# Swapping the first two bank products of each pair in a two-layer graph network kernel

## The chip, the cores and the metric

The kernel runs on one core of one Trainium2 chip. The metric is the device time in microseconds (us) from the first to the last instruction of that core, as the median of several runs. The core has five engines that work side by side and wait for one another through semaphores: TensorE (PE in the profile, its weight loads PEld), VectorE (DVE), ScalarE (ACT), GpSimd (POOL) and SyncE (SP), which issues most of the transfers.

## The reference

Input x is 128 graphs of 64 nodes with 768 features each; `adj` is their 0/1 adjacency. Two layers follow one another, each added to its input. Cut to what matters:

```python
# layer 0: relational graph layer
h = jnp.maximum(_layernorm(x), 0.0)
ctx = jnp.matmul(adj, h @ Wadj.T + badj) / deg            # neighbours
ctx = ctx + jnp.matmul(radj, h @ Wrev.T + brev) / rdeg    # neighbours the other way
ctx = ctx + h @ Wself.T + bself                           # the node itself
rel = agg @ Wr.T + br * deg + ragg @ Wrr.T + brr * rdeg   # sums of relation embeddings
x = x + ctx + rel
# layer 1: graph attention with 6 heads of 128, tanh scores, softmax over neighbours, gate
h = jnp.maximum(_layernorm(x), 0.0)
x = x + gate * elu(attention(h)) + (1 - gate) * h
```

The change touches layer 0 alone, and in it the three products with `Wadj`, `Wrev` and `Wself`.

## The kernel before

The 8192 rows are cut into 64 tiles of 128 rows, and the tiles into 32 pairs. Pass 1 does layer 0 pair by pair, pass 2 does layer 1. In pass 1 the product of a pair (2 tiles by 768 features) with the weights (768 by 768) is split into blocks: 2 tiles by 3 parts of the inner dimension (operands a00 to a12), and 3 by 3 blocks of weights (b00 to b22). Eighteen block products would be needed. The kernel needs fifteen: it forms sums of operands (f1 to f11) and sums of weights (g1 to g14), and adds or subtracts the running content of a PSUM bank to or from the output blocks after each product.

Each line of the table is one product: operand, weights, bank, whether it begins the bank anew, output block, sign, and whether the table products of the relation part are added too. Bank a holds a chain of seven products that is never cleared within a pair; after every product the bank's running sum is read.

```python
PRODUCTS = (
    ("f1", "g6", "a", True, "11", "+", False),
    ("f7", "g10", "b", True, "00", "-", False),
    ("a01", "b11", "d", True, "01", "+", True),
    ("f4", "b21", "a", False, "01", "-", False),
    ("a00", "g12", "b", False, "01", "-", False),
    ("f3", "g8", "c", True, "12", "-", False),
    ("a02", "g14", "a", False, "00", "-", False),
    ("f9", "g9", "b", False, "02", "+", False),
    ("f11", "b10", "d", True, "00", "+", True),
    ("f6", "g5", "a", False, "02", "+", False),
    ("f8", "g3", "b", False, "12", "-", False),
    ("f10", "b12", "c", False, "02", "+", True),
    ("f5", "b22", "a", False, "12", "-", False),
    ("a11", "g1", "b", False, "11", "+", True),
    ("f2", "g11", "a", False, "10", "+", True),
)
# pair 0 uses plain block products instead, in the banks "abcdab", and so ends in bank b
PLAIN = tuple((f"a{k}{j}", f"b{j}{q}", "abcdab"[2 * i + k], j == 0, f"{k}{q}" if j == 2 else None,
               "+", i > 0) for i, q in enumerate((0, 2, 1)) for k in range(2) for j in range(3))
```

How the steps of one pair come about. `psw` is a pool of PSUM tiles with one buffer for each bank's name, so a bank that begins anew must first have been read to the end.

```python
def main(p):
    ...
    def new(b):
        bank[b] = psw.tile([P, 512], F32, name=f"pw{b}")

    def counts(b, c, first=False):          # the table products: two matmuls (L617)
        ...
    def add(b, c, sign="+"):
        ...
        if sign == "+":
            nc.vector.tensor_add(v, bank[b][:, :CQ], v)        # L625
        else:
            nc.vector.tensor_sub(v, v, bank[b][:, :CQ])        # L627

    def product(an, bn, b, first, c, sign, cnt):
        def step(q, s):
            if first and q == s == 0:
                new(b)
            nc.tensor.matmul(bank[b][:, :CQ], OPS[p, an][:, q, s, :], bw[bn][...], ...)   # L633
            if q == KQ - 1 and s == 2 and c:
                if cnt:
                    counts(b, c)
                add(b, c, sign)
        for q in range(KQ):         # 2
            for s in range(3):      # Wadj, Wrev, Wself
                steps.append(lambda q=q, s=s: step(q, s))

    for x in PRODUCTS if p else PLAIN:
        product(*x)

    rest_of = ["12"] if p else ["00", "10"]
    for i, c in enumerate(rest_of):
        b = "dc"[i % 2]
        steps.append(lambda b=b, c=c: (counts(b, c, True), add(b, c)))
    return steps
```

A product is six steps. Other work is put in between by the number of the step, always in the same place in the order of instructions, whichever products stand there:

```python
def beside(p):
    ends = [f for k in range(2) for f in finish(p - 1, k)]
    steps = [(0, lambda: form(p, "f5", "f6", "f3")), (10, lambda: form(p, "f10")),
             (18, lambda: form(p, "f11"))]
    steps += list(zip((32, 40, 49, 55), ends))
    if p == 1:
        steps += [(8, lambda: weights_sums("g9")), (25, lambda: weights_sums("g1")), ...]
    if p + 1 == NP:
        return steps + fetch()      # the last pair: weights of pass 2 are loaded over those of pass 1
    n = p + 1
    return steps + [
        (7, lambda: prep(n)),       # the two casts of the next pair's adjacency
        (13, lambda: devs(n)),
        ...
        (53, lambda: form(n, "f1")),
        ...
        (66, lambda: form(n, "f7", "f4")),
        ...
        (77, lambda: form(n, "f8", "f9", "f2")),
        ...]
```

Each engine runs its instructions in the order in which the program issues them.

Of the kernel before, what the change touches and what calls it, by code (L numbers as in the profile page):

```python
# [53 lines left out]
# [9 lines that stand above are left out]
# [10 lines left out]
PLAIN = tuple((f"a{k}{j}", f"b{j}{q}", "abcdab"[2 * i + k], j == 0, f"{k}{q}" if j == 2 else None,  # L73
               "+", i > 0) for i, q in enumerate((0, 2, 1)) for k in range(2) for j in range(3))
# [58 lines left out]
def kernel(  # L133
# [56 lines left out]
    NP = NT // 2  # L190
# [35 lines left out]
    def merged(main, side):  # L226

        side = sorted(side, key=lambda e: e[0])
        i = 0
        for n, step in enumerate(main):  # L230
            while i < len(side) and side[i][0] <= n:
                side[i][1]()
                i += 1
            step()
        for _, step in side[i:]:
            step()
# [117 lines left out]
    with ExitStack() as px:  # L354
# [249 lines left out]
        def main(p):  # L604

            bank = {}
            steps = []

            def new(b):
                bank[b] = psw.tile([P, 512], F32, name=f"pw{b}")  # L610

            def counts(b, c, first=False):
                k, q = int(c[0]), int(c[1])
                if first:
                    new(b)
                for i, (a, e) in enumerate(PARTS):
                    nc.tensor.matmul(bank[b][:, :CQ], CT_T[p, k][: 3 * (e - a), i, :],  # L617
                                     tabs[i][:, q * CQ : (q + 1) * CQ],
                                     start=(first and i == 0), stop=True, skip_group_check=True)

            def add(b, c, sign="+"):
                k, q = int(c[0]), int(c[1])
                v = X[2 * p + k][:, q * CQ : (q + 1) * CQ]
# [9 lines that stand above are left out]
                    nc.tensor.matmul(  # L633
                        bank[b][:, :CQ], OPS[p, an][:, q, s, :],
                        bw[bn][:, (s * KQ + q) * CQ : (s * KQ + q + 1) * CQ],
                        start=(first and q == s == 0), stop=(q == KQ - 1 and s == 2),
                        skip_group_check=True)
# [4 lines that stand above are left out]
                for q in range(KQ):  # L642
                    for s in range(3):
                        steps.append(lambda q=q, s=s: step(q, s))

            for x in PRODUCTS if p else PLAIN:
                product(*x)

            rest_of = ["12"] if p else ["00", "10"]
# [4 lines that stand above are left out]
# [144 lines left out]
        for p in range(NP):  # L798
            merged(main(p), beside(p) if p else first)
# [436 lines left out]
```

## Time and profile before

| what | value |
|---|---|
| time, median of 3 runs | 2499.7 us (2497.94 to 2507.48) |
| span of the profiled run | 2494.1 us |
| TensorE busy | 2458.7 us, 99% |
| VectorE busy | 1998.9 us, 80% |
| ScalarE busy | 1074.4 us, 43% |
| GpSimd busy | 449.2 us, 18% |
| mean granted TensorE clock | 0.998 |
| busy between 60 and 1500 us, of 1440 | TensorE 1431.2 us, VectorE 1095.0 us |

The profile is one execution, seen by the hardware profiler. Pass 1 takes the first 1500 us or so, pass 2 the rest. In each line of a timeline stand the start, the duration, the engine, the line of the kernel, the operation, and the tiles written and read; several equal instructions in a row are merged into one line with their number. `pwa` to `pwd` are the PSUM banks a to d of pass 1, `op` and `oq` its operands, `x` the rows to which results are added. A matmul of 32-bit data shows as two records. The end of a matmul is modelled, its start is recorded.

### The profile page before, as it was taken

How to read it: one execution, taken by the hardware profiler on the slowest of the kernel's cores; microseconds unless marked ns; L12 is line 12 of the kernel's file. 1: busy time of each engine (PE TensorE's matmuls, PEld its weight loads, DVE VectorE, ACT ScalarE, POOL GpSimd, SP SyncE). 2: the span in 40 equal slices, each digit the busy share in tenths (PEclk: the TensorE clock that was granted, in tenths of full speed). 3: DMA queues.
4: the chain of work that ended last, by engine and by line, in shares of the span. 5: the costliest groups of instructions: out<-in, count | busy, mean ns of one | idle time of the engine just before them, and what ended most of it. 6: DMA issues, size and time to landing. Idle time of an engine off the chain costs nothing. (4 is left out here: it accounts for less than half of the span.)

```text
span 2494.1 us, 35435 instructions
## 1 busy us (share of the span) xinstructions
PE 2458.7 (99%) x12108; PEld 1724.9 (69%) x12108; DVE 1998.9 (80%) x4105; ACT 1074.4 (43%) x3591; POOL 449.2 (18%) x799
## 2 busy tenths in 40 slices
PE   8999999999999999999999999999999999999997
PEld 6888888888888888888888884444444444444445
DVE  8877777777777777777777766888888888888889
ACT  2122122122122222222222224777777777777777
POOL 1112112112111121121121121111111111111122
PEclk9999999999999999999999999999999999999999
DMA  5112112112122122122122154344444444444434
GB/s 178 55 53 106 53 60 100 53 66 93 54 72 87 53 74 85 53 79 81 54 88 72 53 174 140 94 110 111 109 104 110 104 104 104 107 113 105 104 85 100
DMA packets 116215, 224.58 MB, mean 90 GB/s; under 512 B 36554, under 2 KB 49981, under 8 KB 116034
## 3 DMA queue, kind: packets, MB, share of 16 engines
q1 hardware_dynamic: 106162, 197.50, 24.4%
q0 software_dynamic: 9728, 24.78, 6.2%
q8 instruction: 95, 1.56, 0.3%
q14 instruction: 86, 0.70, 0.1%
q10 hardware_dynamic: 144, 0.04, 0.0%
HBM read 96.07 MB, written 100.66 MB: 79 GB/s over the span
## 5 line engine op out<-in xcount | busy, mean ns | idle before, releaser
L633 PE MATMUL pwa<-weights,op 128*128 128x256 f32 x2304 | 548.9, 383 | 10.6 <-DVE x L625 8.8
L633 PEld LDWEIGHTS pwa<-weights,op 128*128 128x128 f32 x2304 | 417.4, 190 | 79.3 <-DVE x L625 17.3
L633 PE MATMUL pwb<-weights,op 128*128 128x256 f32 x1536 | 360.7, 381 | 0.0
L633 PEld LDWEIGHTS pwb<-weights,op 128*128 128x128 f32 x1536 | 289.1, 190 | 44.9 <-issue 6.7
L889 PE MATMUL pma<-weights,op_f 128*128 128x512 f32 x620 | 307.7, 593 | 0.6 <-DVE weights L916 0.6
L286 POOL TENSOR_TENSOR rn<-ve,mhalf 128x1 f32<-128x1 f32 x128 | 93.7, 732 | 948.6 <-DVE ve L285 948.5
L307 DVE TENSOR_TENSOR op<-op 128x768 f32<-128x768 f32 x248 | 241.3, 993 | 1.2
L941 ACT ACTIVATE pr<-pr 128x128 f32<-128x128 f32 x768 | 225.4, 296 | 25.3 <-DVE pr L931 25.2
L483 ACT ACTIVATE h<-x,rn 128x768 f32<-128x768 f32 x64 | 62.4, 1022 | 399.8 <-DVE rn L290 380.9
L663 ACT ACTIVATE hf<-x,rn 128x768 f32<-128x768 f32 x64 | 65.7, 1027 | 353.7 <-issue 250.1
L594 ACT COPY op<-pb 128x768 f32<-128x768 f32 x160 | 121.1, 797 | 180.9 <-PE pb L586 180.3
L889 PE MATMUL pmb<-weights,op_f 128*128 128x512 f32 x372 | 191.2, 595 | 0.0
L889 PEld LDWEIGHTS pma<-weights,op_f 128*128 128x128 f32 x620 | 111.8, 190 | 113.2 <-issue 104.3
L633 PE MATMUL pwc<-weights,op 128*128 128x256 f32 x780 | 187.0, 383 | 0.0
L633 PE MATMUL pwd<-weights,op 128*128 128x256 f32 x768 | 176.3, 379 | 0.0
L633 PEld LDWEIGHTS pwc<-weights,op 128*128 128x128 f32 x780 | 145.6, 190 | 25.2 <-issue 6.7
L665 POOL TENSOR_TENSOR x<-x,hf 128x768 f32<-128x768 f32 x64 | 136.1, 2127 | 134.9 <-ACT hf L663 134.9
L633 PEld LDWEIGHTS pwd<-weights,op 128*128 128x128 f32 x768 | 145.8, 190 | 20.0 <-issue 0.2
L586 PE MATMUL pb<-r,h 64*128 64x192 f32 x1536 | 151.8, 337 | 0.4 <-ACT h L483 0.4
L625 DVE TENSOR_TENSOR x<-pwa,x 128x256 f32<-128x256 f32 x95 | 40.0, 422 | 134.2 <-PE pwa L617 78.4
L586 PEld LDWEIGHTS pb<-r,h 64*128 64x128 f32 x1536 | 122.9, 187 | 33.9 <-issue 22.7
L941 ACT ACTIVATION_READ_ACCUMULATOR pr<-pr 128x1 f32 x768 | 144.4, 188 | 0.0
(207 smaller groups left out, 4337.6 us busy)
## 6 DMA issues: line engine op xcount, KB each, us to landing
x<-in_x_dram SPq DMA_DIRECT2D x64, 384.0 KB
h<-hf SPq DMA_DIRECT2D x64, 384.0 KB
out_dram<-x SPq DMA_DIRECT2D x64, 384.0 KB
hh<-hh SPq DMA_DIRECT2D x64, 384.0 KB
h<-h SPq DMA_DIRECT2D x64, 384.0 KB
x<-hh SPq DMA_DIRECT2D x64, 384.0 KB
out_dram<-f POOLq DMA_DIRECT2D x62, 384.0 KB, 5.0
hx<-weights SPq DMA_DIRECT2D x88, 192.0 KB
```

The source lines that it names most:

```text
L286: nc.gpsimd.tensor_tensor(to[:, 0:1], ve, mhalf, op=OP.pow)
L307: return (nc.vector.tensor_add if s1 == "+" else nc.vector.tensor_sub)(to, x, y)
L483: nc.scalar.activation(h, X[t], AF.Relu, scale=to[:, 0:1], bias=to[:, 1:2])
L586: nc.tensor.matmul(ps[:, g, i * 3 * N : (i + 1) * 3 * N], H0[t][s, kb * P : (kb + 1) * P], rts[p % 2][s, k].rearrange("p s n -> p (s n)"), ...
L594: nc.scalar.copy(a.rearrange("p h s (g n) -> p g (h s) n", g=GT), ps[:, :, : 6 * N].rearrange("p g (x n) -> p g x n", n=N))
L625: nc.vector.tensor_add(v, bank[b][:, :CQ], v)
L633: nc.tensor.matmul(bank[b][:, :CQ], OPS[p, an][:, q, s, :], bw[bn][:, (s * KQ + q) * CQ : (s * KQ + q + 1) * CQ], start=(first and q == s ...
L663: nc.scalar.activation(h, X[t], AF.Relu, scale=to[:, 0:1], bias=to[:, 1:2])
L665: nc.gpsimd.tensor_add(X[t], X[t], h)
L889: nc.tensor.matmul(bank[p, b], OPS[p, an][:, q, :], bw2[bn][:, 2 * q * CQ : 2 * (q + 1) * CQ], start=(first and q == 0), stop=(q == KQ - 1 ...
L941: nc.scalar.activation(PR[t][:, j, h, :], PR[t][:, j, h, :], AF.Copy, accum_out=to)
```

## The change

The first product of a pair goes into bank a and the second into bank b. The pair before has just ended in bank a. The change lets those two products change places, so that bank b comes first, and does so in pairs 1 to 30. Pair 0 has its own table, and the last pair keeps its order, since the loads for pass 2 overwrite the weights g6 as soon as its first product is through. It is meant to give VectorE the length of a product to read bank a before TensorE writes to it again.

```diff
-            for x in PRODUCTS if p else PLAIN:
+
+
+            later = (PRODUCTS[1], PRODUCTS[0], *PRODUCTS[2:]) if p + 1 < NP else PRODUCTS
+            for x in later if p else PLAIN:
                 product(*x)
```

## The prediction

> **What bounds the kernel now.** I began with the page's first part and its slices. TensorE is busy for 2458.7 of 2494.1 us, so the end of the kernel is set by how closely TensorE's work is packed, and only two things can move it: less work for TensorE, or fewer holes between its matmuls. The change keeps every matmul, so I looked for holes. The page's list of costly groups names one that repeats. In each line the last two fields are the group's busy time with the mean of one, then the idle time just before the group and what ended it.
>
> ```profile
> PE 2458.7 (99%) x12108; PEld 1724.9 (69%) x12108; DVE 1998.9 (80%) x4105; ACT 1074.4 (43%) x3591; POOL 449.2 (18%) x799
> ...
> L633 PE MATMUL pwa<-weights,op 128*128 128x256 f32 x2304 | 548.9, 383 | 10.6 <-DVE x L625 8.8
> L633 PEld LDWEIGHTS pwa<-weights,op 128*128 128x128 f32 x2304 | 417.4, 190 | 79.3 <-DVE x L625 17.3
> ```
>
> L633 is the matmul of pass 1's products, L625 is the addition by which VectorE reads a finished bank. Of all of pass 1's matmuls, those into bank a wait, and mostly for one kind of VectorE instruction. The view of waits, asked for TensorE between 60 and 1480 us (pairs 1 to 30 and the ends of their neighbours), has a single line:
>
> ```profile
> PE pwa L633 <- DVE x L625: 8.8, 30, 0.3
> ```
>
> That is the total, the number of waits and the longest: 30 waits of 0.3 us. To see where they fall I read the timeline of TensorE around one boundary between two pairs. The columns are start, duration, line and operation, output and inputs, and in brackets the idle time before.
>
> ```profile
> 720.59 0.39 PE L617 MATMUL pwa<-tab,cntT 126*128 126x256 bf16 x2
> 720.81 0.38 PE L617 MATMUL pwd<-tab,cntT 126*128 126x256 bf16 x2
> 721.49 2.86 PE L633 MATMUL pwa<-weights,op 128*128 128x256 f32 x12 [0.29 <-DVE x L625]
> 724.18 2.75 PE L633 MATMUL pwb<-weights,op 128*128 128x256 f32 x12
> 726.77 2.75 PE L633 MATMUL pwd<-weights,op 128*128 128x256 f32 x12
> 729.36 0.39 PE L617 MATMUL pwd<-tab,cntT 126*128 126x256 bf16 x2
> 729.59 1.03 PE L633 MATMUL pwa<-weights,op 128*128 128x256 f32 x4
> ```
>
> A product is six matmuls, which the trace shows as 12 records. The old pair ends with its product f2 x g11 and two table matmuls into bank a, then two table matmuls into bank d. The new pair's first product, f1 x g6, goes into bank a again, and must wait until VectorE has read that bank. The next product, f7 x g10 into b, waits for nothing. VectorE over the same time:
>
> ```profile
> 721.01 0.42 DVE L625 TENSOR_TENSOR x<-pwa,x 128x256 f32<-128x256 f32 x1 [2.56 <-PE pwa L617]
> 721.35 0.41 DVE L625 TENSOR_TENSOR x<-pwd,x 128x256 f32<-128x256 f32 x1
> 721.68 0.95 DVE L305 SCALAR_TENSOR_TENSOR op<-op 128x768 f32<-128x768 f32 x1
> 722.66 1.83 DVE L307 TENSOR_TENSOR op<-op 128x768 f32<-128x768 f32 x2
> 724.41 0.42 DVE L625 TENSOR_TENSOR x<-pwa,x 128x256 f32<-128x256 f32 x1
> 724.81 0.29 DVE L488 CAST af<-ai 128x256 f32<-128x256 int32 x1
> 725.14 0.29 DVE L490 CAST ab<-af 128x256 bf16<-128x256 f32 x1
> 725.35 0.95 DVE L307 TENSOR_TENSOR op<-op 128x768 f32<-128x768 f32 x1
> 726.97 0.42 DVE L627 TENSOR_TENSOR x<-x,pwb 128x256 f32<-128x256 f32 x1 [0.67 <-PE pwb L633]
> ```
>
> VectorE was idle for 2.56 us before it read bank a at 721.01, so it is not late: the wait is the length of its own read (0.42 us) and the signals on both sides, of which the two table matmuls into d cover only 0.22 us.
>
> **What the Trainium skill says.** "PSUM — Partial Sum Buffer", section "PSUM bank collisions raise a hardware error", says that two engines must not use one bank and quadrant of partitions at once, at whichever addresses, and that the program must guard it with semaphores by bank. So the wait cannot just be dropped; another bank must be worked on meanwhile, which is the change. The trace agrees in so far as TensorE resumes at 721.49, after the read's 721.43. "TensorE: Matmul & The Clock Gate", section "Step-by-step: what each phase is for", says that weight loads are pulled ahead of running matmuls and that the drain of one matmul overlaps the fill of the next, so a wait costs more than the hole one sees. The trace agrees: the hole is 0.29 us, but the weight loads waited 17.3 us over 30 times, 0.58 us each. Section "HAM oscillation — how this bites in real kernels" of the same page puts the idle gap that slows the clock at about 3.4 us. Here gaps are 0.3 us and the granted clock is 0.998, so I count no gain from the clock.
>
> **The change part by part.** No instruction is added or removed. For pairs 1 to 30 the first product goes into b and the second into a.
>
> What one wait costs, from starts. With no wait, the two table matmuls and the next product's start are 729.59 - 729.36 = 0.23 us apart, and a product takes 726.77 - 724.18 = 2.59 us to the start of the next. At the boundary the two distances are 721.49 - 720.81 = 0.68 and 724.18 - 721.49 = 2.69 us. So 0.45 us are lost ahead of the product and 0.10 us inside it, because its first weight load could not run beside earlier work: 0.55 us in all. The boundary to the last pair shows the same: 1464.98 - 1461.61 = 3.37 us from the table matmuls into d to the second product, as 724.18 - 720.81 = 3.37 here, against 0.23 + 2.59 = 2.82.
>
> Where it goes away. The 30 waits are at the starts of pairs 2 to 31. The last pair, 31, keeps its order, so 29 waits go: 29 x 0.55 = 16.0 us.
>
> What is there in its place for bank b. It was last read at 718.03 (0.42 us), well before 721.03, when f7 x g10 can now start. Its operand f7 was formed at about 755 to 757 us in the cycle before the boundary at 767.79, some 11 us ahead, so no operand is missing.
>
> Where it costs. Pair 0 has another order of banks: it ends in bank b, with four table matmuls into d and c behind it. There the present order is the free one and the new one waits:
>
> ```profile
> 72.95 0.38 PE L617 MATMUL pwd<-tab,cntT 126*128 126x256 bf16 x2
> 73.17 0.39 PE L617 MATMUL pwc<-tab,cntT 126*128 126x256 bf16 x2
> 73.39 2.75 PE L633 MATMUL pwa<-weights,op 128*128 128x256 f32 x12
> ```
>
> VectorE reads b at 73.34. At the other boundary TensorE resumed 721.49 - 721.01 = 0.48 us after such a read began, which here gives 73.82, 0.43 us later than 73.39; with the 0.10 us inside the product the cost is 0.53 us, once.
>
> What moves later. Bank a's second product of the pair, f4 x b21 (729.59 here), must wait for the read of f1 x g6, and that read moves from first to second place on VectorE. With the swap, f7 x g10 ends at about 723.6 and is read at about 724.4, when VectorE is through with its three formed operands (the read of bank a stood there before). f1 x g6 runs from 723.6 to about 726.2. VectorE comes from its casts and one more formed operand at about 726.3, reads a, and is done by 726.9. The product f4 x b21 is due at 729.0. Two microseconds are left. In pair 1 an extra sum of weights (1.75 us) stands between the two reads: bank b was read there at 80.45 to 80.86, and bank a will be instead, against a start of f4 x b21 near 81.9. About one microsecond is left.
>
> Sum: 16.0 - 0.5 = 15.5 us of TensorE's path. VectorE has 23% to 25% idle in this pass (1095.0 of 1440.0 us busy between 60 and 1500) and sits waiting for TensorE before most of its reads, so it follows a TensorE that is 0.55 us a pair earlier. Pass 2 is the same program and only starts sooner. 2499.7 - 15.5 = 2484.2 us.
>
> **The rivals.**
> The first: only the visible holes go, 29 x 0.29 = 8.5 us, and 2491 us remain. For it speaks that busy time on TensorE is modelled; against it that starts are recorded and give 0.55 us twice over.
> The second: the wait moves to f4 x b21, since bank a now has one product less between its two uses. For it speaks that VectorE reads it in order behind operands and casts. Against it stand the 2 us of slack above; it would need VectorE to be 2 us later than now. If it came true in all pairs, the gain would shrink towards nothing and the time would stay at 2500.
> The third: TensorE comes so early that an operand or a buffer from ScalarE or VectorE becomes its bound, say the three formed operands at the pair's start. Against it: TensorE now waits for nothing else in these pairs, and the first of the three is used in the sixth product, more than 10 us after the boundary. It would cost a few tenths a pair, ending near 2490.
>
> **Range and chances.** The sum of 15.5 us has an error of perhaps 1 us from reading starts to 0.01 us at a few boundaries. Most of the range is the spread of runs: 2497.94, 2499.7 and 2507.48 before. A median of the changed kernel may sit 3 us either side, and I leave more room above for a part of the rivals: 2479.5 to 2490.5. A change of 2% is 50 us, more than three times all that the removed waits hold, so within 2% is nearly certain.
>
> **What would show it right or wrong.** Right: TensorE's wait for L625 falls from 30 times to about two (start of pair 1 on bank b, start of pair 31 on bank a), some 0.6 us in all, and the weight loads' wait falls from 17.3 us to about 1.2. A pair takes 45.75 us instead of 46.30 ((1462.29 - 721.49) / 16). The starts at a boundary stand 0.23 us and 2.59 us apart. Wrong: a new wait for L625 before the fourth product, a wait of the same size on bank b at each boundary, or a pair that keeps 46.3 us without a hole that one can see. A drop of the granted clock below 0.998 would also spoil it.

## The result and the profile after

The changed kernel takes 2484.24 us (median of 4 runs, 2481.44 to 2486.32) against 2501.7 us for the kernel before in the same series (the three runs given above and a fourth at 2503.71). The ratio is 0.9927 with a 95% interval of 0.9904 to 0.9951, which is 12 to 24 us less. 2484.2 us was predicted. Three later series of the kernel before, of 28, 20 and 9 runs, have medians of 2498.96, 2499.61 and 2499.79 us. Two of the four runs before lie above 2503 us, but only 11 of these 57, so the gain is more likely 15 than 17 us. (The description of the kernel above speaks of seven products in bank a; its table has six.)

From the page of the changed kernel: TensorE's share, and the groups of matmuls and weight loads of bank a, now with bank b's beside them.

```profile
PE 2455.3 (99%) x12108; PEld 1727.7 (70%) x12108; DVE 1998.9 (80%) x4105; ACT 1074.4 (43%) x3591; POOL 449.9 (18%) x799
...
L633 PE MATMUL pwa<-weights,op 128*128 128x256 f32 x2304 | 547.7, 382 | 3.7 <-DVE x L627 3.4
L633 PEld LDWEIGHTS pwa<-weights,op 128*128 128x128 f32 x2304 | 420.9, 190 | 66.7 <-issue 7.6
...
L633 PE MATMUL pwb<-weights,op 128*128 128x256 f32 x1536 | 360.8, 381 | 0.3 <-DVE x L625 0.3
```

Bank a's 8.8 us behind L625 are gone from its group. What is left there is a single wait of 3.4 us behind another line, L627, and L625 no longer ends most of the idle time of bank a's weight loads. The view of waits for TensorE between 60 and 1480 us has two lines now:

```profile
PE pwa L633 <- DVE x L625: 0.3, 1, 0.3
PE pwb L633 <- DVE x L625: 0.3, 1, 0.3
```

They are the start of the last pair, which keeps its order, and the start of pair 1, where the new order waits. TensorE's timeline at a boundary between two pairs:

```profile
714.07 0.39 PE L617 MATMUL pwd<-tab,cntT 126*128 126x256 bf16 x2
714.29 2.75 PE L633 MATMUL pwb<-weights,op 128*128 128x256 f32 x12
716.88 2.75 PE L633 MATMUL pwa<-weights,op 128*128 128x256 f32 x12
...
722.06 0.39 PE L617 MATMUL pwd<-tab,cntT 126*128 126x256 bf16 x2
722.28 1.03 PE L633 MATMUL pwa<-weights,op 128*128 128x256 f32 x4
```

The first product starts 0.22 us after the table matmuls and gives way to the next after 2.59 us: 2.81 us where it was 3.37 us. VectorE beside it:

```profile
714.26 0.42 DVE L625 TENSOR_TENSOR x<-pwa,x 128x256 f32<-128x256 f32 x1 [2.56 <-PE pwa L617]
...
717.66 0.41 DVE L627 TENSOR_TENSOR x<-x,pwb 128x256 f32<-128x256 f32 x1
...
719.67 0.42 DVE L625 TENSOR_TENSOR x<-pwa,x 128x256 f32<-128x256 f32 x1 [0.19 <-PE pwa L633]
720.01 1.01 DVE L282 BATCH_NORM_STATS2 st<-x 128x6 f32<-128x384 f32 x2
```

The read of the old pair's bank a still starts as soon as its table matmuls are through, but TensorE works in bank b meanwhile. The read of the new a is over at 720.09; f4 x b21 needs bank a at 722.28. The start of pair 1 shows the price:

```profile
73.17 0.38 PE L617 MATMUL pwc<-tab,cntT 126*128 126x256 bf16 x2
73.83 2.86 PE L633 MATMUL pwb<-weights,op 128*128 128x256 f32 x12 [0.27 <-DVE x L625]
```

The product starts at 73.83 instead of 73.39 us, and takes 2.69 us to the next one's start (76.52).

Where the time went, by landmarks. The first stretch runs from the last two table matmuls of pair 0 to the first product of pair 31, the second from there to the first product of pass 2 into its bank d (`pmd`), both from starts in the timelines of one profile. The medians come from four series of runs (the changed kernel; the next three; the four with sums or tail up to tail_sums; tail_sums_w), and each ratio is against the kernel before in the same series, so kernels of different series are compared by their ratios. The names of the rows are those of the experiments below.

| kernel | median us | ratio, 95% interval | pairs 1 to 30, us | last pair, us |
|---|---|---|---|---|
| before | 2501.7 | 1 | 1462.29 - 73.17 = 1389.12 | 1506.37 - 1462.29 = 44.08 |
| changed | 2484.24 | 0.9927 (0.9904 to 0.9951) | 1446.58 - 73.17 = 1373.41 | 1494.30 - 1446.58 = 47.72 |
| d_first | 2511.52 | 1.005 (1.0034 to 1.0067) | 1399.51 | 48.60 |
| devs_early | 2499.35 | 1.0005 (0.9996 to 1.0014) | 1387.37 | 49.79 |
| half | 2491.46 | 0.997 (0.9962 to 0.9978) | 1380.70 | 46.25 |
| before_sums | 2495.42 | 0.9986 (0.9978 to 0.9993) | 1389.11 | 42.01 |
| after_sums | 2479.5 | 0.9924 (0.9912 to 0.9937) | 1373.39 | 41.85 |
| tail | 2484.11 | 0.9938 (0.9925 to 0.9951) | 1372.43 | 45.32 |
| tail_sums | 2478.51 | 0.9913 (0.99 to 0.9927) | 1372.42 | 43.09 |
| tail_sums_w | 2478.27 | 0.992 (0.9906 to 0.9933) | 1372.42 | 41.91 |
| before, second and third profile | | | 1389.11, 1389.11 | 45.03, 44.54 |
| changed, second and third profile | | | 1373.41, 1373.42 | 45.86, 46.44 |

The first stretch repeats to 0.02 us from profile to profile, the second does not. The change took 15.71 us from the first stretch. In these two profiles the last pair gave 3.64 us back, so pass 2 began 12.07 us earlier. Pass 2 keeps this lead until some 22 us before its end (a matmul at 2472.05 us before is at 2459.98 us after), and 1.7 us go in those last 22 us, where the granted clock was 0.50 for longer (from 2461.20 us, for 10.24 us, in place of 3.41 us, and in both kernels again in the last 7.47 us). That leaves the 10.4 us between the two spans (2494.1 and 2483.7).

### The profile page after: what moved, and what is told of

Read it like the earlier page. It is cut to its first block, busy times and chain, and to the rows that moved or that the text cites. A ratio compares the mean times of both kernels' runs of the same rounds, so it can differ in the third digit from the quotient of the medians.

```text
span 2483.7 us, 35435 instructions
## 1 busy us (share of the span) xinstructions
PE 2455.3 (99%) x12108; PEld 1727.7 (70%) x12108; DVE 1998.9 (80%) x4105; ACT 1074.4 (43%) x3591; POOL 449.9 (18%) x799
## 5 line engine op out<-in xcount | busy, mean ns | idle before, releaser
L625 DVE TENSOR_TENSOR x<-pwa,x 128x256 f32<-128x256 f32 x95 | 40.3, 424 | 142.0 <-PE pwa L617 80.1
```

## The experiments

My theory: TensorE waits for nothing but the read of the bank that it is about to begin, each wait costs 0.55 us although only 0.29 us of it is seen as idle, and the change removes 29 of them. The rivals: the visible 0.29 us is the whole cost (the prediction's 8.5 us is 29 of 30 parts of the 8.8 us in the view of waits; 29 x 0.29 is 8.4); any other first product would do as well; VectorE has room for anything.

**Half of the pairs** (half). The swap in pairs 2, 4, ... 30 alone.

```diff
-            later = (PRODUCTS[1], PRODUCTS[0], *PRODUCTS[2:]) if p + 1 < NP else PRODUCTS
+            later = (PRODUCTS[1], PRODUCTS[0], *PRODUCTS[2:]) if p % 2 == 0 else PRODUCTS
```

> The swap only in pairs 2, 4, ... 30. Theory (0.55 us for each wait taken away, each boundary for itself): 15 waits go, none is added, 8.2 us less than before up to the start of the last pair, and about as much in the whole. Rival (a wait costs the 0.29 us that one sees as idle): 4.4 us less. In the trace the start of the last pair settles it to 0.1 us.

The first stretch is 8.42 us shorter than before: 15 waits at 0.56 us. In the changed kernel it is 15.71 us for 29 waits less the 0.54 us of pair 1, again 0.56 us each. The visible idle alone would have given 15 x 0.29 = 4.4 us. The whole kernel is 0.3% faster (0.9962 to 0.9978, or 5.5 to 9.5 us). This profile's own span, 2495.6 us, must not be set beside the others: the start of pair 1 came 5.9 us later in it, because the first matmuls of the kernel ran at half the pace for longer. The line shows two matmuls of the start-up (four records) in the profile of half; in the kernel before they took 1.52 us.

```profile
11.31 2.85 PE L458 MATMUL pb<-wrt,es 128*81 128x384 f32 x4
```

**Another first product** (d_first). The product into bank d comes first.

```diff
-            later = (PRODUCTS[1], PRODUCTS[0], *PRODUCTS[2:]) if p + 1 < NP else PRODUCTS
+            later = (PRODUCTS[2], PRODUCTS[0], PRODUCTS[1], *PRODUCTS[3:]) if p + 1 < NP else PRODUCTS
```

> Pairs 1 to 30 begin with the product a01 x b11 into bank d, then f1 x g6 (a), then f7 x g10 (b). Theory (the wait belongs to the bank, and lasts until VectorE has read that bank): bank d was written by the last table matmuls of the old pair and is read at the second place on VectorE, 0.34 us after bank a, so TensorE starts 0.48 us after that read begins: 0.80 us later than with a free bank and 0.10 us lost inside the product, 0.90 us a pair against 0.55 us before. In all about 29 x 0.35 + 1 = 11 us slower than the kernel before. Rival (it is enough that the first product isn't one into bank a, the bank of the last product): as fast as the changed kernel, 15 us faster than before.

TensorE's timeline of this kernel at a boundary:

```profile
726.16 0.38 PE L617 MATMUL pwd<-tab,cntT 126*128 126x256 bf16 x2
727.17 2.86 PE L633 MATMUL pwd<-weights,op 128*128 128x256 f32 x12 [0.62 <-DVE x L625]
```

The wait is there, on bank d, and longer: 1.01 us from the table matmuls to the product instead of 0.68 before. VectorE began to read bank d at 726.70, and TensorE resumed 0.47 us later. The first stretch is 10.39 us longer than before, as the theory has it (11 us); the whole is 0.5% slower. So it is not enough to begin elsewhere than in a. What counts is whether VectorE has already read what was last written to the bank.

**The room that is left** (devs_early). The changed kernel, with the statistics moved ahead of bank a's read.

```diff
-                (13, lambda: devs(n)),
+                (11, lambda: devs(n)),
```

> The changed kernel, with the two tiles' statistics (2.72 us on VectorE) put ahead of the read of the second product instead of behind it. Theory (bank a's read has 2.2 us to spare before f4 x b21): the read of a ends 0.3 us after f4 x b21 is due, which costs 0.3 us and 0.1 us inside the product, 0.4 us a pair and 1.9 us in pair 1, where a sum of weights stands there too: 13 us slower than the changed kernel, 2 to 3 us faster than before. Rival (VectorE has more slack than that, since it is idle a quarter of the time): no difference from the changed kernel.

The line of TensorE's timeline at which f4 x b21 now starts, 0.53 us after the table matmuls at 729.26 instead of 0.22 us:

```profile
729.79 1.13 PE L633 MATMUL pwa<-weights,op 128*128 128x256 f32 x4 [0.15 <-DVE x L625]
```

VectorE's read of bank a runs from 729.31 to 729.73 there. The first stretch is 13.96 us longer than in the changed kernel, of which 13 us were expected: 2.7 us more between the two reads use up the 2.2 us of room and take back almost all of the gain, while only 5.9 us of waiting are seen in the view of waits. VectorE's idle quarter did not help, since it lies elsewhere in the pair.

**The last pair.** The 3.4 us wait in the changed kernel is TensorE's last product of pass 1 (f2 x g11, bank a), which waits for the read that follows bank a's product before it, f5 x b22, two products earlier. Here first TensorE's line, then VectorE's, in the changed kernel:

```profile
1488.14 4.54 PE L633 MATMUL pwa<-weights,op 128*128 128x256 f32 x12 [3.40 <-DVE x L627]
```

```profile
1482.67 2.48 DVE L307 TENSOR_TENSOR weights<-weights 128x1024 f32<-128x1024 f32 x2 [2.62 <-DMA weights<-in_hw_t_dram]
...
1487.68 0.41 DVE L627 TENSOR_TENSOR x<-x,pwa 128x256 f32<-128x256 f32 x1
```

VectorE stood idle for 2.62 us before a sum of weights whose load had not landed; the read of bank a was behind it in order. Four kernels bear on this: before_sums and after_sums, the kernel before and the changed kernel with some of the last pair's sums moved behind the reads; tail, with another cure for the boundary wait; and tail_sums, with both. The edit of the sums:

```diff
-                    (59, "g5"), (65, "v"), (67, "g3"), (70, "g9"), (73, "g1"), (76, "g8"),
-                    (79, "g11"))])
+                    (60, "g5"), (65, "v"), (78, "g3"), (79, "g9"), (84, "g1"), (76, "g8"),
+                    (84, "g11"))])
```

> The kernel before, with four of the last pair's sums of weights for pass 2 (g3, g9, g1, g11) moved behind the read of the thirteenth product, and g5 behind the read of the tenth. Theory (in the last pair VectorE stands in order behind a sum whose weights are still being loaded, and TensorE's last product waits for a read behind it, 1.75 us before the change): that wait goes, 1.9 us less than before. Rival (the sums are needed so early in pass 2 that the wait returns there): no difference.

This is before_sums. The last pair takes 42.01 us in place of 44.08 us, and no wait for L627 is left; the median falls by 4.2 us, with an interval of 0.07% to 0.22%, or 1.8 to 5.5 us. The expected 1.9 us lies at its edge.

> The changed kernel with the same sums moved. Theory (the loads of the last pair do not come earlier by as much as TensorE does, so the wait grew from 1.75 to 3.40 us, another 0.3 us was lost before the thirteenth product, and behind the long wait the clock fell and the last product took 1.7 us more): all three go, the last product follows at once and its clock stays at 1.0, 5 us less than the changed kernel's profile, and 17 to 18 us less than before. Rival (the loss is made by the transfers and only moves into pass 2): no difference from the changed kernel.

TensorE's last product of pass 1 in after_sums:

```profile
1483.97 2.75 PE L633 MATMUL pwa<-weights,op 128*128 128x256 f32 x12
```

The last product follows at once and runs at its usual pace. The last pair falls from 47.72 to 41.85 us, the kernel to 2479.5 us, by the ratio 19 us under the kernel before (16 to 22 us). The rival, that the loss only moves into pass 2, falls. Against before_sums, in the same series, after_sums is 15.9 us faster (2495.42 and 2479.50), its first stretch is 15.72 us shorter, and from pair 1 to the end its profile is 15.9 us shorter too: once the last pair's wait for loads is gone from both kernels, the whole of the swap's gain reaches the end. The reason that I had written for the growth of the wait is another matter, below.

The other cure (tail) lets the pair end in bank b, so that the first products need not change.

```diff
-            for x in PRODUCTS if p else PLAIN:
+            ends_in_b = (*PRODUCTS[:11], *(PRODUCTS[k] for k in (12, 11, 14, 13)))
+            for x in ends_in_b if p else PLAIN:
```

> The kernel before with another cure for the same wait: the first products keep their order, and the end of each pair 1 to 31 is ordered f5 x b22 (a), f10 x b12 (c), f2 x g11 (a), a11 x g1 (b), so that a pair ends in bank b. Theory (only the distance between a bank's last product and its next first product counts): all 30 waits go, none is added at pair 1 since pair 0 ends in b too; the last pair starts 16.5 us earlier than before, 0.8 us earlier than in the changed kernel, and the total is within 2 us of the changed kernel's because the last pair's wait for loads remains. Rival (a and a lie closer together at the end of the pair now, so the wait moves in front of f2 x g11): no gain, or a loss of up to 0.5 us a pair.

TensorE's timeline of this kernel at the start of the last pair:

```profile
1445.45 0.39 PE L617 MATMUL pwd<-tab,cntT 126*128 126x256 bf16 x2
1445.68 2.75 PE L633 MATMUL pwa<-weights,op 128*128 128x256 f32 x12
```

All 30 boundary waits are gone, the last pair's too, and the first stretch is 1372.43 us, 16.69 us less than before and 0.98 us less than in the changed kernel. The product f1 x g6 comes first here as it did before, and no longer waits, so its operands and weights were not the cause. Of the rival's wait before f2 x g11 nothing is seen in these pairs; the last pair shows one of 0.34 us. That pair, 45.32 us, now waits 2.2 us at its twelfth product, for a read behind a sum whose load had not landed. The median of 2484.11 us is 15.5 us less than before by the ratio.

> Both: the pair's end reordered, and the last pair's sums moved. Theory: 16.5 us of boundaries and 1.9 us of the last pair, 18.4 us less than before and the fastest of the four. Rival: the last pair's loads give back 3 to 5 us as in the changed kernel.

tail_sums takes 2478.51 us, 21.7 us less than before by the ratio (18 to 25 us): the lower of the two kernels with moved sums by 1 us, within their intervals. In the last pair 1.1 us of waiting was left, again behind a sum that stood in order before a read. A last kernel (tail_sums_w) moves that too.

```diff
-                    ... (50, "g14"), (57, "w"),
+                    ... (50, "g14"), (60, "w"),
```

> The reordered end of the pair and the moved sums, with the sum w moved behind the read of the tenth product too. Theory (the 1.07 us wait that was left in the last pair is for that read, which stands in order behind w and its load): the wait goes, the last pair takes 41.9 us instead of 43.1 us, 1.2 us less in the whole. Rival (w is needed soon after, by the sums of the last products, so another wait of the same size appears): no difference.

The wait is gone and the last pair takes 41.91 us as expected, but the median, 2478.27 us, does not show it: 1 us is below what these series resolve.

**Does the swap lengthen the last pair?** In the table the last pair is longer not only in the changed kernel but also in d_first, where TensorE is later than before. That speaks against what I had written, that TensorE ran ahead of the loads. Both kernels were profiled twice more, unedited.

> The kernel before, unchanged, profiled once more. The last pair of pass 1 (from its first product to pass 2's first product) took 44.08 us before and 47.72 us after, and 46.25 to 49.79 us in three other kernels in which TensorE was early or late alike. Theory A (when the last pair's loads land differs from execution to execution): the kernel before shows another value, by a microsecond or more, at a new profile. Theory B (the swap lengthens the last pair, because TensorE is ahead of the loads): about 44.1 us again. The stretch from the start of pair 1 to the start of pair 31 is 1389.1 us again in both.

> The changed kernel, unchanged, profiled once more. Theory A: a last pair of anything between 44 and 50 us, not tied to the swap. Theory B: 47 to 48 us again. From the start of pair 1 to the start of pair 31: 1373.4 us again in both.

> The kernel before, a third profile. As for the second: theory A another value of the last pair, theory B 44.1 us.

> The changed kernel, a third profile. As for the second: theory A anything between 44 and 50 us, theory B 47 to 48 us.

TensorE's wait before its last product was 1.75, 2.69 and 2.05 us in the three profiles of the kernel before, and 3.40, 1.85 and 2.42 us in those of the changed kernel. The two ranges overlap, so the length of this wait comes mostly from when the loads land in that execution (theory A), and three profiles each can't show a small part of the swap in it. Neither theory was met to the letter: the kernel before came back 0.95 and 0.46 us longer, where theory A asked for a microsecond or more, and the changed kernel at 45.86 and 46.44 us, where theory B asked for 47 to 48.

In all three profiles of the changed kernel, though, the last product itself was slow, and in none of the kernel before. These are its lines in the first two profiles of the kernel before, then in the second of the changed kernel:

```profile
1501.90 2.86 PE L633 MATMUL pwa<-weights,op 128*128 128x256 f32 x12 [1.75 <-DVE x L627]
```

```profile
1502.44 2.86 PE L633 MATMUL pwa<-weights,op 128*128 128x256 f32 x12 [2.69 <-DVE x L627]
```

```profile
1486.00 4.24 PE L633 MATMUL pwa<-weights,op 128*128 128x256 f32 x12 [1.85 <-DVE x L627]
```

And these are lines of the view by stretches for that product, first of the changed kernel, then of the kernel before; the third value from the end is the mean granted clock of TensorE.

```profile
1488.10:1492.60 4.50, 4.46 (x13) 3.55 (x14) 1.46 (x2) 0.00 (x0) 0.00 (x0) 0.62 0.00 0
```

```profile
1501.90:1504.70 2.80, 2.80 (x13) 2.39 (x14) 1.41 (x2) 0.00 (x0) 0.00 (x0) 1.00 0.00 0
```

In the changed kernel the clock was low in that product (0.62, 0.66 and 0.60) and it took 4.24 to 4.54 us; in the kernel before it was 1.00 and the product took 2.86 us. Half, d_first and devs_early had the low clock too. The length of the wait ahead of it does not separate them: 1.85 us was followed by a low clock and 2.69 us was not.

The clock records of the same traces show what does. In each profile the granted clock is 1.00 or 0.50 from its first record on, and all its changes lie on one grid of 3.413 us. In the changed kernel, for example, it falls at 1488.40 us, rises at 1491.82 and falls again at 2461.20, which are 1 and 284 steps. Where the grid lies differs from execution to execution; in the kernel before it can be laid back from the changes at the end of pass 2. A step is the time between two neighbouring lines of the grid. The table gives each wait of more than 1.5 us in the last pair, how much of TensorE's idle time then fell into a single step (the largest share), and the clock granted in the step that followed.

| profile | wait, us | idle in one step, us | clock next |
|---|---|---|---|
| before | 1.75 | 1.75 | 1.00 |
| before, second | 2.69 | 1.37 (and 1.32 in the step before it) | 1.00 |
| before, third | 2.05 | 1.81 | 1.00 |
| tail | 2.22 | 1.80 | 1.00 |
| changed | 3.40 | 3.15 | 0.50 |
| changed, second | 1.85 | 1.85 | 0.50 |
| changed, third | 2.42 | 2.42 | 0.50 |
| half | 2.07 | 2.07 | 0.50 |
| d_first | 3.76 | 2.04 | 0.50 |
| devs_early | 4.49 | 3.41 | 0.50 |

So what decides is how a wait falls on the grid: the wait of 2.69 us is cut in two, that of 1.85 us lies in one step. The border, between 1.81 and 1.85 us here, fits every step at full clock after the first 60 us in all fourteen profiles, the end of pass 2 included, where the nearest steps are 1.83 us (full clock next) and 1.98 us (half). It is read from traces, in part from modelled ends of matmuls, and no run was made to move a wait along the grid, so it is a rule found afterwards and not tested. But it leaves no reason to charge the slow product to the swap. What six profiles show is a last pair that waits for loads, by an amount and at a place on the grid that change from execution to execution; that the swap lengthens it is not shown.

## Why the prediction was right, step by step

- **What one wait costs, 0.55 us.** Right: 0.56 us in half, in the changed kernel and in tail, from 15, 29 and 30 waits. The hole of 0.29 us that is seen as idle is about half of it.
- **29 waits go.** Right: two of 0.3 us are left in pass 1 up to the last pair, at the two places named.
- **Bank b is free and f7 ready.** Right: from pair 2 on the product starts 0.22 us after the table matmuls.
- **Pair 1 pays 0.53 us.** Right: it starts 0.44 us later and its first product takes 0.10 us more, 0.54 us.
- **Two microseconds are left before f4 x b21, one in pair 1.** Right: 2.2 us in the changed kernel, and devs_early shows what happens when they are used up. In pair 1 bank a's read ended at 80.89, f4 x b21 started at 81.92.
- **The sum, 15.5 us.** Measured from pair 1 to pair 31: 15.71 us. A pair takes 45.74 us (45.75 forecast), and the weight loads' wait for L625 fell from 17.3 to 1.5 us (1.2 forecast). The three rivals fall: the first by half, the second and third because no other wait appeared in pairs 2 to 30.
- **Pass 2 only starts sooner.** This step is incomplete. The last pair of pass 1 had a wait behind loads already in the kernel before (1.75 us), which the prediction left out, since its view of waits ended at 1480 us. In the changed kernel's three profiles that pair was 0.8 to 3.6 us longer, whichever of the three of the kernel before one sets beside it, mostly by the low clock of its last product (1.4 to 1.7 us), which fits where the waits fell on the clock's grid and not the swap. Pass 2 itself took 987.7 to 989.4 us in the three profiles before and 988.4 to 989.9 us in the three after, so it repeats to about 2 us only. From pair 1 to the end the changed kernel's profiles are on average 12.8 us shorter: 15.7 less 2.1 in the last pair and 0.8 in pass 2.
- **The total.** The 15.5 us were subtracted from 2499.7 us, while the kernel before measured 2501.7 us in the series of the result, a fall of 17.5 us with an interval of 12 to 24. That 2484.24 us came so near to 2484.2 is therefore luck; that a fall of this size came is not, since the first stretch and the pair of before_sums and after_sums show it.

The clock was named as what could spoil it, "a drop of the granted clock below 0.998". As a sign this was badly chosen: the changed kernel shows 0.996 to 0.997, but most runs of the kernel before do too, and 0.998 was a high value among them.

## What to carry to other kernels

Where products write to few accumulator banks in turn, look at the distance between the last use of a bank and its next beginning, across the border of the loop too: reading a bank takes its time even when the reading engine is idle, and another bank's product in between hides it. Price such a wait by the starts of the instructions around it and not by the idle time that the profile gives, and count in which iterations the neighbours differ. When TensorE is at 99%, check also what stands in order ahead of a read on the engine that releases it; here one sum that waited for a load held up the last product of a whole pass.

## What was not expected of the hardware

A wait of 0.29 us of visible idle cost 0.56 us. The gap of about 3.4 us that slows the clock, which the prediction took from the Trainium skill ("TensorE: Matmul & The Clock Gate", section "HAM oscillation — how this bites in real kernels"), is not what these traces show: the clock fell after a wait of 1.85 us and not after one of 2.69 us, by how much of the wait lay in one step of a grid of 3.413 us. The start of the kernel differs by 5.8 us between two executions of the changed kernel, by how long the first matmuls run at half the pace: the two start-up matmuls shown above took 2.85 us in two profiles (half and the third of the changed kernel), whose first record of full clock is at 22.86 and 22.12 us, and 1.52 us in the other twelve, where it is at 9.3 to 10.9 us.
